# A state-space decoder layer: one GpSimd product for both half states, and a residual added by TensorE

## The chip, the cores and the metric

The kernel runs on one core of a Trainium2 chip. The metric is the device time of one execution in microseconds (us). The time before is the median of three runs; beside it there is one profiled execution, whose trace gives the times of single instructions. The core has five engines with a queue of instructions each: TensorE (PE, with its weight loads, PEld), VectorE (DVE), ScalarE (ACT), GpSimd (POOL) and SyncE (SP, which here issues DMA transfers). An engine works through its queue in order; it waits for another engine by a semaphore.

## What is computed

One decoder layer on x (4 sequences of 512 tokens, 256 channels) and a context of the same shape, all float32: a state-space network of two layers, cross-attention with 16 heads, and a mixture of 8 experts (the best 2 per token) beside a shared feed-forward part, each added to the stream.

```python
x = x + ssm(layernorm(x))
x = x + cross_attention(layernorm(x), ctx)
x = x + moe_and_shared(layernorm(x))

# one ssm layer; B and C have 16 states, xb has 512 channels
def scan_fn(carry, inp):
    h, v = carry
    dA_t, mi_t, C_t = inp
    v = BETA * v + mi_t            # BETA = 0.6
    h = dA_t * h + v
    return (h, v), jnp.einsum('ben,bn->be', h, C_t)
...
y = (y + dp * xb) * silu(z)
return jnp.einsum('ble,de->bld', y, ow)     # added to the layer's input
```

Here dA = exp(delta * A) and mi = delta * B * xb, for each of 512 channels, 16 states and 512 tokens of a sequence. The change touches the product of h with C, its sum over the states, and the last addition of the second layer: its output, the first layer's, and the x from outside.

## The kernel before

**Phases.** The state-space phase runs from the kernel's start to about 1214 us, the attention to about 1500, the experts to the end. Only the first is changed. In it, the stream of all four sequences stays in SBUF as `xs`, and the order of instructions is written out by hand (the function carries `manual_schedule`): what each engine's queue holds, and in what order, is the order in the program.

**Steps, pairs, units.** The work is cut into 8 steps, one for each layer and sequence: first layer 0 with its four sequences, then layer 1. Each step has 4 blocks of 128 channels (e), each block 2 pairs (q = 0 and 2), so there are 64 pairs. A pair covers two quarters of 32 channels (j = 0, 1). The 128 partitions of a tile hold 4 groups of 32: the same 32 channels with four of the 16 states. Four indices n = 0..3 thus make up the 16 states. A pair is 5 units, in an order given by the string `TURNS` (L59; "ffhfh" in four pairs of a step, then "fhfhf" in three, "hfhff" in the last).

- An *f* unit is a whole: one n from 1 to 3 with both quarters, in tiles of 128x1024 (two times 512 tokens). ScalarE makes the decay exp(delta * A) (L693), GpSimd the drive m = dxs * B (L702), VectorE scans v = 0.6 v + m into PSUM (L738) and then h = decay * h + v into SBUF (L747). GpSimd multiplies h by C in place (L760).
- An *h* unit is a half: n = 0 with one quarter, 128x512. Here v is not scanned. TensorE makes it as a product with a band of powers of 0.6 (`filtered`, 40 small products at L720) in the single PSUM buffer `vf`, and VectorE scans `hh` from it (L735). GpSimd multiplies it by C (L760 too). The half with js == (0,) is called `early`; the other one follows two units later.

Each f or each pair of halves ends as two products of TensorE with `joined` (L774), which add the four groups of states into the 32 rows of y in PSUM. TensorE does them one unit after the product with C or later: `sums` empties the list `pending`, and holds it back in the first units of each block until the block before has been gated (`finished`, L787: z = y * z on VectorE).

**Order within a unit.** The main loop's body is: decay of three groups ahead (ScalarE), drive of two wholes ahead (GpSimd), scans (VectorE), product with C (GpSimd), the bands' products for the unit two ahead, a piece of a background generator, the sums of what is pending (TensorE). The background generator is the next step's prologue: norm, input projection (L383), convolution (L499), the small matrices, the softplus. Where a projection is open, it goes before the background.

**Buffers.** m, h and hh are taken from the pool `ring3`, three buffers under each name. The tile framework makes a scan wait until the readers of the buffer that it gets are done.

**Projections.** After a step's last block has been gated, `projected` (L796 to L818) is done in the first units of the next step, in two rounds of two blocks of 128 tokens each. A round is eight products of TensorE into the PSUM tile `po` (L807; the trace has 16 records for them), then VectorE's cur += po (L816) on the stream's slice `cur`. In layer 1, GpSimd then adds the x from outside: cur += xt (L818). `xt` is loaded by SP at L802, when the projection begins, into a buffer shared with the softplus (`pre1`, tag "w"). In this phase layer 1 is projected for sequences 0 to 2, in the steps that begin at about 784, 924 and 1064 us; sequence 3's projection is done in the attention's code, which the change does not touch. `ident` is the 128x128 identity matrix, which the prologue uses for transposes and sums.

Of the kernel before, what the change touches and what calls it, by code (L numbers as in the profile page):

```python
# [10 lines left out]
F32 = mybir.dt.float32  # L11
I32 = mybir.dt.int32
AF = mybir.ActivationFunctionType
ALU = mybir.AluOpType
# [3 lines left out]
P = 128  # L18
B, L, D = 4, 512, 256
KD = D // P  # L20
TB = L // P
NL = 2
# [45 lines left out]
def decoder_layer(  # L68
# [26 lines left out]
    nc = tc.nc  # L95
# [7 lines left out]
    ident = const.tile([P, P], F32, name="ident")  # L103
# [106 lines left out]
    with ExitStack() as ph:  # L210
# [7 lines left out]
        pre6 = ph.enter_context(tc.tile_pool(name="ssm_pre6", bufs=6))  # L218
        ring2 = ph.enter_context(tc.tile_pool(name="ssm_ring2", bufs=2))
        ring3 = ph.enter_context(tc.tile_pool(name="ssm_ring3", bufs=3))  # L220
        ps_beta = ph.enter_context(tc.tile_pool(name="ssm_ps_beta", bufs=1, space=PSUM))
        ps_v = ph.enter_context(tc.tile_pool(name="ssm_ps_v", bufs=1, space=PSUM))
        ps_vf = ph.enter_context(tc.tile_pool(name="ssm_ps_vf", bufs=1, space=PSUM))
# [439 lines left out]
        for i in range(len(pairs)):  # L663
            ns, js = iter(range(1, SQ)), iter(((0,), (1,)))
# [42 lines left out]
        left = []  # L707

        filtering = {}

        def filtered(u):

# [16 lines left out]
        def scanned(u):  # L729
            i, n, js = units[u]  # L730
            dA = decaying[i, n][:, js[0] : js[-1] + 1, :]
            if n == 0:
                v = filtering.pop(u)
                h = ring3.tile([P, L], F32, name="hh")
                nc.vector.tensor_tensor_scan(h, dA[:, 0, :], v, 0.0, ALU.mult, ALU.add)  # L735
                return h.unsqueeze(1)
            v = ps_v.tile([P, 2, L], F32, name="v")
            nc.vector.tensor_tensor_scan(  # L738
                v.rearrange("p n t -> p (n t)"),
                beta.rearrange("p n t -> p (n t)"),  # L740
                entering.pop(u).rearrange("p n t -> p (n t)"),
                0.0,
                ALU.mult,
                ALU.add,
            )
            h = ring3.tile([P, 2, L], F32, name="h")
            nc.vector.tensor_tensor_scan(  # L747
                h.rearrange("p n t -> p (n t)"),
                dA.rearrange("p n t -> p (n t)"),
                v.rearrange("p n t -> p (n t)"),  # L750
                0.0,
                ALU.mult,
                ALU.add,
            )
            return h

        def weighted(u, h):
            i, n, js = units[u]
            Cs = made[pairs[i][0]][3][1]
            nc.gpsimd.tensor_tensor(h, h, Cs[n].unsqueeze(1).to_broadcast([P, len(js), L]), ALU.mult)  # L760
            return h

        def summed(u, *hcs):
# [32 lines left out]
        def projected(s, z):  # L796

            l, b = s
            outw = weights[l][5][0]
            if l == NL - 1:  # L800
                xt = pre1.tile([P, TB, D], F32, tag="w", name="xt")
                nc.sync.dma_start(xt, blocks(x[b]))  # L802
            for t in range(0, TB, 2):
                po = ps.tile([P, 2, D], F32, tag="mm", name="po")
                for i in range(2):
                    for k in range(NE):
                        nc.tensor.matmul(  # L807
                            po[:, i, :],
                            z[k // 2][:, k % 2, (t + i) * P : (t + i + 1) * P],
                            outw[:, k, :],  # L810
                            start=(k == 0),
                            stop=(k == NE - 1),
                        )
                yield
                cur = xs[:, b, t : t + 2, :]
                nc.vector.tensor_tensor(cur, cur, po, ALU.add)  # L816
                if l == NL - 1:
                    nc.gpsimd.tensor_tensor(cur, cur, xt[:, t : t + 2, :], ALU.add)  # L818


        DOUBLE = (8, 23, 38), (8, 13, 18, 23, 30, 33, 38)
# [23 lines left out]
        pending = []  # L845
# [74 lines left out]
        for u, (i, n, js) in enumerate(units):  # L920
            s, e, q = pairs[i]
            if u % 16 == 15 and empty < NX * ROWS + SPARE * P:
                empty = emptied(empty)
            if u % 16 == 7:
                next(fillers, None)
            if u % per == 0 and (e, q) == (0, 0):
                k = steps.index(s)
                if k == 0:
                    background = chained(background, prologue(*steps[1], s))
                    foreground = None  # L930
                else:
                    for _ in background:
                        pass
                    if s == (1, 0):
                        load_others(1)
                    if k + 1 < len(steps):
                        background, foreground = prologue(*steps[k + 1], s), None
                    else:
                        background, foreground = kept_from(), gates(s)

                fetching = k > 0 and k + 1 < len(steps) and steps[k + 1][0] == 0
                if fetching:
                    next(background)
                slot = 0
            if s == (1, 0) and slot == 10:
                load_last(1)
            if u in groups and groups.index(u) + LEAD < len(groups):
                later = groups[groups.index(u) + LEAD]
                i2 = units[later][0]
                if later % per == 0 and i2 + 1 < len(pairs):  # L950
                    while pairs[i2 + 1] not in stored:
                        next(background)
                    copied(i2 + 1)
                owed.append(later)
            between = units[u - 1][1:] == (0, (0,))
            while owed and not between and (n > 0 or 0 in js):
                decayed(owed.pop())
            if n > 0 and wholes.index(u) + AHEAD < len(wholes):
                driven(wholes[wholes.index(u) + AHEAD])
            gating = 3 if TURNS[i // 2 * 2 % len(TURNS)][1] == "h" else 2  # L960
            if u % per == gating and q == 0 and u > per:
                finished(*pairs[i - 1][:2])
            h = scanned(u)
            if projections:

                if n > 0 and next(projections[0], s) is s:
                    projections.pop()
            elif slot > 1 and foreground is not None:
                if next(foreground, s) is s:
                    foreground = None  # L970
            early = n == 0 and js == (0,)
            hc = weighted(u, h)

            def filters():
                if u + 2 < len(units) and units[u + 2][1] == 0:
                    s2, e2 = pairs[units[u + 2][0]][:2]
                    while (s2, e2 // 2) not in ready:
                        next(background)
                    filtered(u + 2)

            def sums():

                while pending and not 0 < slot % (2 * per) < gating:
                    summed(*pending.pop(0))

            if early:
                filters()
                sums()
                half = hc[:, 0, :]
            else:  # L990
                if n > 0:
                    filters()
                if 0 < slot <= 4 or not projections and foreground is None and not (fetching and slot == 0):
                    held = next(background, None)
                    if held is None and not projections and (
                        n > 0 and (k == 0 and slot < 20 or k == len(steps) - 1 or units[(u + 1) % len(units)][1] > 0) or slot in DOUBLE[k < len(steps) - 1]
                    ):
                        next(background, None)
                if n == 0:
                    filters()  # L1000
                sums()
                pending.append((u, hc[:, 0, :], hc[:, 1, :]) if n > 0 else (u, half, hc[:, 0, :]))
            if k + 1 < len(steps) and slot in (36, 38):
                spread(steps[k + 1], 0 if slot == 36 else 3)
            if slot == 36 and k + 1 < len(steps):
                bands = banded()
            if slot >= 36 and k + 1 < len(steps):
                for _ in range(2):
                    next(bands, None)
            slot += 1  # L1010
# [263 lines left out]
    with ExitStack() as ph:  # L1274
# [20 lines left out]
        for i in range(2):  # L1295

            t = wp.tile([P, TB, P], F32, name=f"tops{i}")
# [10 lines left out]
        xt = ring.tile([P, TB, D], F32, tag="wide", name="xt")  # L1308
# [74 lines left out]
        n = B * NG * 8  # L1383
        for s in range(-LEAD, n + 2):
            u, k = divmod(s, 8)
# [72 lines left out]
    with ExitStack() as ph:  # L1458
# [174 lines left out]
        for b in range(B):  # L1633
            for c in range(TOP):
                first = NB * P + (c * B + b) * L
                n = TB * D
# [20 lines left out]
        halves = {b: shared(b) for b in (2, 3)}  # L1657
# [70 lines left out]
```

## Time and profile before

| What | Value |
|---|---|
| median of 3 runs | 1793.54 us (1793.04 to 1795.99) |
| profiled execution | 1796.24 us, of which the span of its instructions is 1794.5 |
| mean granted TensorE clock | 0.938 |
| state-space phase | 60 to about 1214 us; 8 steps of about 140 us |
| GpSimd, h * C, 128x1024 (L760) | 192 times, 2361 ns each |
| GpSimd, hh * C, 128x512 (L760) | 128 times, 1279 ns each |
| GpSimd, m = dxs * B, 128x1024 (L702) | 192 times, 2365 ns each |
| GpSimd, cur += xt, 128x512 (L818) | 6 times, 1275 ns each |
| VectorE, scans of v and of h, 128x1024 | 192 times each, 2281 and 2287 ns |
| VectorE, scan of hh, 128x512 (L735) | 128 times, 1205 ns each |
| VectorE, cur += po (L816) | 14 times, 689 ns each |
| TensorE, y with joined (L774) | 768 records, 629 ns each, for h and hh together |
| TensorE, po (L807) | 224 records, 379 ns each |

The page of a profile shows an execution from several sides: the busy share of each engine, the span in 40 slices, the chain of work that ended last, and groups of equal instructions. A group is written `out<-in`, with partitions x elements; the number behind `x` is how often it occurs, then come its busy time and the mean of one. "Idle before" is the time in which the engine stood still just ahead of these instructions, and the name behind the arrow is what ended it. A line of waits, `A <- B`, reads: A waited, and B's end released it. Busy times of products on TensorE overlap, since they are pipelined; how long a group of them takes is read from its first start to its last end.

### The profile page before, as it was taken

To read this page: it belongs to the slowest core of one execution; us is meant where nothing else is said; L and a number is where in the kernel's file an instruction comes from. 1 tells how busy PE (TensorE), PEld (TensorE's weight loads), DVE (VectorE), ACT (ScalarE), POOL (GpSimd) and SP (SyncE) were. 2 spreads that over 40 slices of the span, in tenths; PEclk is the share of its full clock that TensorE was granted. 3 is DMA by queue.
4 is the path that set the end of the run, shared out by engine and by line. 5 is a ranking of instruction groups with operands and counts; after the bars stand their busy time and mean duration, and the time that the engine had idled before them with its cause. 6 is when DMAs were issued, how large, how long until landed. Compare 5 with 4: busy or idle time off the path is not lost.

```text
span 1794.5 us, 28198 instructions
## 1 busy us (share of the span) xinstructions
PE 1564.6 (87%) x10666; PEld 736.6 (41%) x10666; DVE 1386.3 (77%) x1260; ACT 1028.3 (57%) x1613; POOL 1241.9 (69%) x781
## 2 busy tenths in 40 slices
PE   6679789779879879879979968877999999899998
PEld 2234343334334334334434334433233333466665
DVE  3588899989999999999999999985567676432223
ACT  4658767747876866876776765531444444412221
POOL 5598899989989999999999999982000211245540
PEclk9889999989999989989989989997999999899999
DMA  3433543543553653634554443633310100532214
GB/s 80 141 91 96 141 107 96 128 103 97 132 136 70 152 140 90 156 100 101 143 131 97 126 122 97 170 93 120 118 48 24 59 9 16 162 104 64 65 59 153
DMA packets 122991, 185.71 MB, mean 103 GB/s; under 512 B 19464, under 2 KB 58248, under 8 KB 122856
## 3 DMA queue, kind: packets, MB, share of 16 engines
q1 hardware_dynamic: 117576, 169.45, 35.9%
q0 software_dynamic: 5280, 14.46, 2.5%
q8 instruction: 85, 1.39, 0.3%
q14 instruction: 50, 0.41, 0.1%
HBM read 124.38 MB, written 59.46 MB: 102 GB/s over the span
## 4 chain that ended last, share of the span: by engine, by line
PE 58%; DVE 18%; ACT 10%; issue 7%; POOL 5%; DMA 2%; SPq 1%; DVEq 0%; another core or an unknown queue 0%; POOLq 0%; ACTq 0%
DVE v L738 8%; PE y L774 6%; PE sT L1424 6%; PE pc L499 5%; PE pp L383 5%; DVE h L747 5%; PE vf L720 4%; PE pu L1578 4%; PE sum L581 4%; PE pw L1601 4%; PE o L1337 3%; ACT decay L693 3%; PE sc L1424 3%; POOL h L760 2%; PE y L770 2%
## 5 line engine op out<-in xcount | busy, mean ns | idle before, releaser
L760 POOL TENSOR_TENSOR h<-h,Cs 128x1024 f32<-128x1024 f32 x192 | 453.3, 2361 | 53.3 <-DVE h L747 42.3
L702 POOL TENSOR_TENSOR m<-dxs,Bs 128x1024 f32<-128x1024 f32 x192 | 453.9, 2365 | 16.6 <-DMA deltas<-wide 16.6
L747 DVE TENSOR_TENSOR_SCAN h<-decay,v 128x1024 f32<-128x1024 f32 x192 | 439.1, 2287 | 17.7 <-DVE v L738 1.0
L738 DVE TENSOR_TENSOR_SCAN v<-beta,m 128x1024 f32<-128x1024 f32 x192 | 438.0, 2281 | 15.3 <-POOL m L702 10.4
L693 ACT ACTIVATE decay<-deltas,scaleA 128x511 f32<-128x511 f32 x512 | 332.7, 714 | 59.9 <-DVE h L747 58.9
L720 PE MATMUL vf<-band,dxT 106*32 106x102 f32 (+1 forms) x5120 | 184.2, 269 | 86.5 <-DVE hh L735 85.7
L1430 DVE TENSOR_REDUCE tops<-sc 128x2 f32<-128x1024 f32 x128 | 156.4, 1225 | 98.9 <-PE sc L1424 91.4
L774 PE MATMUL y<-h,joined 128*32 128x512 f32 x768 | 205.3, 629 | 27.3 <-POOL h L760 27.0
L720 PEld LDWEIGHTS vf<-band,dxT 106*32 106x32 f32 (+1 forms) x5120 | 145.4, 116 | 161.9 <-issue 110.9
L1435 ACT ACTIVATE at<-sT 128x1024 f32<-128x1024 f32 x128 | 128.8, 1024 | 140.1 <-PE sc L1424 100.1
L735 DVE TENSOR_TENSOR_SCAN hh<-decay,vf 128x512 f32<-128x512 f32 x128 | 154.2, 1205 | 29.2 <-PE vf L720 29.2
L760 POOL TENSOR_TENSOR hh<-hh,Cs 128x512 f32<-128x512 f32 x128 | 163.7, 1279 | 8.7 <-DVE hh L735 8.5
L113 POOL TENSOR_TENSOR rstd<-ve,neghalf 128x4 f32<-128x4 f32 x12 | 12.3, 1027 | 207.4 <-DVE ve L111 207.4
L1424 PE MATMUL sc<-kpad,qpad 32*128 32x512 f32 x512 | 145.1, 664 | 7.2 <-ACT at L1435 4.8
L1424 PE MATMUL sT<-q,kpad 32*128 32x512 f32 x512 | 139.1, 657 | 3.3 <-DVE q L1329 3.3
L383 PE MATMUL pp<-xnT,inw 128*128 128x512 f32 x256 | 124.1, 622 | 6.9 <-ACT z L658 3.4
L499 PE MATMUL pc<-xpad,taps 128*128 128x512 f32 x240 | 112.1, 604 | 0.0
L1610 POOL DMA_INDIRECT rows_out<-yg,target x39 | 40.0, 1026 | 78.8 <-DVE xgT L1571 68.6
L774 PEld LDWEIGHTS y<-h,joined 128*32 128x32 f32 x768 | 34.4, 112 | 137.4 <-issue 70.7
L1205 POOL DMA_INDIRECT rows_in<-row,at x32 | 31.8, 994 | 82.3 <-DVE stat L1218 39.6
L693 ACT ACT_TABLE_LOAD x62 | 79.5, 1283 | 5.2 <-DMA deltas<-wide 4.1
L1594 DVE COPY hgT<-pf 128x512 f32<-128x512 f32 x39 | 27.0, 692 | 69.1 <-PE pf L1592 69.1
(254 smaller groups left out, 2316.2 us busy)
## 6 DMA issues: line engine op xcount, KB each, us to landing
dxs<-wide SPq DMA_DIRECT2D x256, 128.0 KB
deltas<-wide SPq DMA_DIRECT2D x256, 128.0 KB
rows_in<-nothing SPq DMA_DIRECT2D x17, 1028.0 KB
Cs<-rows SPq DMA_DIRECT2D x128, 64.0 KB
wide<-w SPq DMA_DIRECT2D x16, 512.0 KB
wide<-ln SPq DMA_DIRECT2D x16, 512.0 KB
Bs<-rows SPq DMA_DIRECT2D x32, 192.0 KB
xt<-in_x_dram SPq DMA_DIRECT2D x8, 512.0 KB
```

The costliest lines, as they stand in the source:

```text
L383: nc.tensor.matmul(pp, weights[l][1][half][:, k, m * P : (m + 1) * P], xnT[:, k, :], start=(k == 0), stop=(k == KD - 1),)
L499: nc.tensor.matmul(pcs[j], taps[:, e, k, :], xpads[j][:, k : k + L], start=(k == 0), stop=(k == KC - 1),)
L693: nc.scalar.activation(dA[:, j, 1:], copies[i][0][:, j, 1:], AF.Exp, scale=weights[s[0]][6][:, e, q + j, n : n + 1])
L702: nc.gpsimd.tensor_tensor(m, copies[i][1], Bs[:, n - 1, :].unsqueeze(1).to_broadcast([P, 2, L]), ALU.mult)
L720: nc.tensor.matmul(v[r * QP : (r + 1) * QP, CHUNKS[c] : CHUNKS[c + 1]], made[s][5][e // 2][:k, c, first : first + QP], band[:k, c, r, : CH ...
L735: nc.vector.tensor_tensor_scan(h, dA[:, 0, :], v, 0.0, ALU.mult, ALU.add)
L738: nc.vector.tensor_tensor_scan(v.rearrange("p n t -> p (n t)"), beta.rearrange("p n t -> p (n t)"), entering.pop(u).rearrange("p n t -> p ...
L747: nc.vector.tensor_tensor_scan(h.rearrange("p n t -> p (n t)"), dA.rearrange("p n t -> p (n t)"), v.rearrange("p n t -> p (n t)"), 0.0, AL ...
L760: nc.gpsimd.tensor_tensor(h, h, Cs[n].unsqueeze(1).to_broadcast([P, len(js), L]), ALU.mult)
L774: nc.tensor.matmul(ys[s, e][(q + j) * QP : (q + j + 1) * QP, :], joined, hcs[j], start=False, stop=(u % per == per - 1),)
L1424: nc.tensor.matmul(o, l, m, start=True, stop=True)
L1430: nc.vector.tensor_reduce(top[:, t2, 2 * h : 2 * h + 2, HD : HD + 1], sc, AX.X, ALU.max, negate=True)
```

## The change

It has two parts.

1. The two half states of a pair go into the two halves of one tile `h` (128x2x512). Each half's scan writes its half; GpSimd multiplies nothing after the first, and the whole tile by C after the second. Tiles of halves and of wholes come from one pool `ring4` of four buffers with a common tag, instead of three for wholes and three for halves. The sums read the two halves of that tile.
2. In layer 1's projections in this phase, TensorE adds x to the sum in `po`: for each block of 128 tokens a product of `ident` with the block of `xt` goes first into the group. VectorE's addition of `po` to the stream stays, GpSimd's addition is gone.

```diff
+        ring4 = ph.enter_context(tc.tile_pool(name="ssm_ring4", bufs=4))
...
+        halves = {}
...
             if n == 0:
                 v = filtering.pop(u)
-                h = ring3.tile([P, L], F32, name="hh")
-                nc.vector.tensor_tensor_scan(h, dA[:, 0, :], v, 0.0, ALU.mult, ALU.add)
-                return h.unsqueeze(1)
+                if 0 in js:
+                    halves[i] = ring4.tile([P, 2, L], F32, tag="h", name="hh")
+                h = halves[i]
+                nc.vector.tensor_tensor_scan(h[:, js[0], :], dA[:, 0, :], v, 0.0, ALU.mult, ALU.add)
+                return h
...
-            h = ring3.tile([P, 2, L], F32, name="h")
+            h = ring4.tile([P, 2, L], F32, tag="h", name="h")
...
-            nc.gpsimd.tensor_tensor(h, h, Cs[n].unsqueeze(1).to_broadcast([P, len(js), L]), ALU.mult)
+            nc.gpsimd.tensor_tensor(h, h, Cs[n].unsqueeze(1).to_broadcast([P, 2, L]), ALU.mult)
...
                 for i in range(2):
+                    if l == NL - 1:
+
+                        nc.tensor.matmul(po[:, i, :], ident, xt[:, t + i, :], start=True, stop=False)
                     for k in range(NE):
                         nc.tensor.matmul(
...
-                            start=(k == 0),
+                            start=(k == 0 and l < NL - 1),
...
                 nc.vector.tensor_tensor(cur, cur, po, ALU.add)
-                if l == NL - 1:
-                    nc.gpsimd.tensor_tensor(cur, cur, xt[:, t : t + 2, :], ALU.add)
...
-            hc = weighted(u, h)
+
+            hc = h if early else weighted(u, h)
...
-                half = hc[:, 0, :]
...
-                pending.append((u, hc[:, 0, :], hc[:, 1, :]) if n > 0 else (u, half, hc[:, 0, :]))
+                pending.append((u, hc[:, 0, :], hc[:, 1, :]))
```

## The prediction

> **What bounds the kernel now.** I read the page first, then the waits by engine over the stretch that the change touches, then the chain of waits in one step, then the instructions in order of time around one projection.
>
> ```profile
> PE 1564.6 (87%) x10666; PEld 736.6 (41%) x10666; DVE 1386.3 (77%) x1260; ACT 1028.3 (57%) x1613; POOL 1241.9 (69%) x781
> ```
>
> Over the span no engine is full, but the state-space phase (60 to 1214 us) is 64% of it and has 64 pairs in 8 steps of 140 us. There GpSimd looks like the bound: 145.8 of 150 us busy between 690 and 840 us, with VectorE at 143.2 and TensorE at 130.9. The waits say otherwise. This is GpSimd from 540 to 1140 us:
>
> ```profile
> engine line waited for: us in total, times, longest us
> POOL h L760 <- DVE h L747: 16.0, 24, 1.7
> POOL hh L760 <- DVE hh L735: 1.0, 1, 1.0
> ```
>
> and this is VectorE over the same 600 us:
>
> ```profile
> engine line waited for: us in total, times, longest us
> DVE hh L735 <- PE vf L720: 10.3, 15, 1.1
> DVE z L787 <- PE y L774: 3.7, 4, 1.4
> DVE xs L816 <- PE po L807: 3.0, 5, 1.1
> DVE w L606 <- PE sum L581: 1.2, 4, 0.4
> DVE v L738 <- POOL m L702: 0.5, 1, 0.5
> ```
>
> GpSimd catches VectorE up and waits for it (17 us). VectorE waits for GpSimd 0.5 us, and for TensorE 18 us. So GpSimd is full, and follows; VectorE and TensorE set the pace in turns. The chain of waits for 656 to 705 us shows TensorE's turn:
>
> ```profile
> by line: PE y L774 22.3%; PE pp L383 21.8%; PE pc L499 17.0%; PE vf L720 15.0%; PE po L807 14.9%; PE y L770 6.2%; DVE hh L735 2.5%; PE pt L474 2.1%; issue 0.6%
> ...
> 663.35 3.65 PE po L807 x16
> 669.70 3.65 PE po L807 x16
> ```
>
> In a step TensorE first waits 7 to 10 us for a scan, then runs without a gap, and VectorE stops for it again and again (hh L735, z L787, xs L816). The projections, po, lie in just this stretch. In the step's second part TensorE waits for VectorE (vf L720 <- DVE hh, 3.0 to 3.2 us), and VectorE paces.
>
> **Part 1: one product for both halves.** Per pair GpSimd loses two products of 1.279 us and gets one of 2.361 (L760): 64 x (2.558 - 2.361) = 12.6 us less work. The engine that loses it is the one that waits for others, so I put this at nothing, with one exception. TensorE waits for a weighted state in a few places of its own stretch (0.89 us at 527.9, 0.58 at 816.9, 0.51 at 956.7), where GpSimd is late because of the first half's product, the small operations of the norm and L818. Those waits close. In layer 1's first step GpSimd works back to back from 521.9 us, the first half's 1.28 comes off and the second half's 1.08 goes on soon after, so only 0.2 remains. With as much in step 0, the gain is 0.4 us. The other two count in part 2.
>
> The cost is lateness: a pair's second half is ready 2.36 us after GpSimd begins instead of 1.28. Behind it in GpSimd's queue stand the next m and h; the m is made two scans ahead (it is ready 5 to 9 us early), and the sum on TensorE comes late anyway: the product that ended at 704 us would end at about 705, its counterpart in the next step at 805.1 was summed at 812.4. Nobody waits.
>
> At the phase's end nothing moves either: the last h is scanned to 1209.9, GpSimd waits 2.5 us for it, and no half is left.
>
> A page speaks for more. The Trainium skill (SBUF — State Buffer, "SBUF: two separate sides") says that GpSimd and VectorE share a pair of ports as an exclusive lock, which the later one waits for until the holder's instruction ends. Were it so here, freeing GpSimd would quicken the scans. The row:
>
> ```profile
> L747 DVE TENSOR_TENSOR_SCAN h<-decay,v x192: 2286/2287/2290, 64.0 to 1207.6; 128x1024 f32<-128x1024 f32 x192
> ```
>
> Shortest, median and longest lie within 4 ns, and the 1202.78 scan, during 1.87 us of GpSimd's idleness, took 2.29 as well. By the rule up to 12.6 us; by the row nothing. I take nothing (each scan takes one input from PSUM, so the rule's own condition, two SBUF inputs, isn't met).
>
> **Part 1, the buffers.** The half states move into the four buffers of the whole states. A scan must wait until the sum that last read its buffer has ended. In the kernel before, a pool hands out the buffer whose last reader comes first in the program (the addresses in the compiled program show it for the exponentials of L1434, which are read last in another order than they are made). With this order I went through all 256 uses against the times of the sums: the sums end 1 to 5 us early, except at the last pair of each step, where the first half's scan would wait 0.25 to 0.58 us (scan 765.82, sum of F1 in pair 6 ended 766.30). The same half's partner waits 1.1 us for vf at 772.73, which hides it: nothing.
>
> What stays are the waits as instructions. The start of h after v differs by what it waits for:
>
> ```profile
> 703.01 2.30 DVE L738 TENSOR_TENSOR_SCAN v<-beta,m 128x1024 f32<-128x1024 f32 x1
> 705.45 2.29 DVE L747 TENSOR_TENSOR_SCAN h<-decay,v 128x1024 f32<-128x1024 f32 x1
> 707.65 1.20 DVE L735 TENSOR_TENSOR_SCAN hh<-decay,vf 128x512 f32<-128x512 f32 x1
> 708.76 2.27 DVE L738 TENSOR_TENSOR_SCAN v<-beta,m 128x1024 f32<-128x1024 f32 x1
> 711.07 2.29 DVE L747 TENSOR_TENSOR_SCAN h<-decay,v 128x1024 f32<-128x1024 f32 x1
> ```
>
> 2.44 us start to start where h also waits on ScalarE and TensorE, 2.31 where on v alone. Over the phase the medians are 2.307 (v alone), 2.376 (ScalarE too), 2.430 (both), 2.402 (TensorE without ScalarE): TensorE's wait costs 0.054 to 0.095. 64 of 192 h have it. A state whose buffer was a half's must wait for a sum that stands behind the last vf already waited for, some 5 times a step: about 40 more, 2.2 to 3.8 us. Here too a page speaks against the row: VectorE: DVE Perf Modes, "The DRAIN you can't avoid", measured no cost of a semaphore after each operation; by it the sum is 0. The row measures this wait, so I take it; but half falls where VectorE waits for TensorE anyway. I take 1.6; ends 0 and 3.8.
>
> **Part 2: x through TensorE.** GpSimd loses six additions of 1.276 us (7.7 us, off the path as above). TensorE gets one product of 128x256 per block of tokens, with ident: 4 for each of the 3 batches projected in this phase. The row nearest is po itself: 16 records, 8 products, in 3.72 us, thus 0.465 each. Two go into each po: +0.93 us per po, +1.86 per step. VectorE's addition keeps its length and now follows a longer po. TensorE also waits for x, which formerly GpSimd read later. The loads land at 797.3, 937.7 and 1083.6, the products would start at 801.5, 941.3 and 1084.2: no wait, by 0.6 us in the third; if it were lost, some tenths. SP issues the same load in the same place.
>
> Does the stretch hide the 1.86? At step 5:
>
> ```profile
> 806.06 0.66 DVE L816 TENSOR_TENSOR xs<-xs,po 128x512 f32<-128x512 f32 x1
> ...
> 811.57 0.69 DVE L816 TENSOR_TENSOR xs<-xs,po 128x512 f32<-128x512 f32 x1 [0.24 <-PE po L807]
> 812.69 1.22 DVE L735 TENSOR_TENSOR_SCAN hh<-decay,vf 128x512 f32<-128x512 f32 x1 [0.43 <-PE vf L720]
> ```
>
> The first addition has nearly 0.9 us to spare (po ended 805.18), the second none: it and the hh behind it, whose vf is queued behind po, move by 1.86. Then TensorE wins back its wait for GpSimd (0.58): 1.28 stay. From 817 to 855.9 TensorE has no gap over 0.2 us; ScalarE waits there for it (3.7 us) and runs on without a gap, and VectorE waits for them (0.89, 0.73, 0.64, 0.45). So 1.28 arrive where VectorE takes over, and nothing wins them back. Step 6: 1.86 - 0.51 = 1.35. Step 7: its first po costs 0.53 (TensorE's next transposes waited 0.68 for the addition anyway), its second 0.93: 1.46. Sum 4.1; ends 0, were every wait elastic, and 5.6.
>
> **Sum.** 4.1 + 1.6 - 0.4 = +5.3 us. The profiled execution took 1796.24 us (span 1794.5 and 1.7 around it), so it would take 1801.5; the median of the runs is 2.7 lower: 1793.54 + 5.3 = 1798.8.
>
> **Rivals.** *GpSimd is the bound after all.* Its 97% speaks for it, its waits against. All of its work that goes would count: 12.6 + 7.7 = 20.3 us, 1773. Chance 0.10.
>
> *Everything is absorbed.* For it speaks that ScalarE's wait of 3.7 us after the projection could take up the 1.28, if VectorE's stops for ScalarE behind it didn't grow with it; against it that VectorE already stops four times for TensorE and ScalarE in that stretch, each time with less to spare. Of the sum the waits as instructions stay at half their value, 0.8 to 1: 1794.5, between 1791 and 1797. Chance 0.27.
>
> *The buffers stop VectorE (much slower).* If the four buffers are handed out in turn, a first half gets the half's buffer of the pair before, whose sum TensorE does late. From the trace the scans would wait 0.7 to 1.8 us in the first part of a step (scan at 723.30, sum ended 725.05) and 2.2 to 2.5 in its last pair (769.33 against 771.77). TensorE comes back to VectorE's pace between the two, so both count: some 4 us in each of 8 steps, +32: 1826. It decides as soon as a sum ends after the scan four buffers later. Against it stands the order shown above. Chance 0.08.
>
> **Numbers.** The forecast has 0.55, own range 1795.5 to 1804. A measurement of this kernel tells about 0.2% (3.6 us) from no change, thus 1790 to 1797.1. Faster: the first rival 0.10 and 0.02 of the second, 0.12. Same: 0.25 of the second and 0.10 of the forecast's lower end, 0.35. Slower: 0.45 of the forecast and the third rival's 0.08, 0.53. The range 1790 to 1806 leaves out the first and third rivals.
>
> **What would show it.** Right: L774 waits for h less at 817 and 957; L816's wait grows by about 1.9 us per step in layer 1; GpSimd's waits for h L747 grow by some 10 us over the phase; steps 0 to 4 keep 140 us within 0.5. Wrong: h L747 or the half scans waiting 1 us and more for y L774 (buffers), VectorE waiting for GpSimd, steps 0 to 4 shorter by 1.5 us (GpSimd bound), or po waiting for x.

## The result, and the profile after

The changed kernel takes 1806.58 us, the median of 7 runs (1801.15 to 1809.84), against 1793.57 for the kernel before (7 runs, 1793.04 to 1796.27). The ratio, taken over the runs of both, is 1.0064, 95% interval 1.0052 to 1.0075: 11.5 us slower, 9.3 to 13.5, thus about 1805.1. (The two medians lie 13.0 apart; what follows goes by the ratio.) The forecast was +5.3, 1798.8. The result lies at the upper edge of the stated range, 1790 to 1806, and above the forecast's own range, which ended at 1804. The direction was right, the size less than half. The profiled execution took 1806.58, with a span of 1804.9. In the code after, lines have moved by 1 to 7: L764 is h * C, L751, L742 and L739 are the scans of h, v and hh, L778 the sums, L814 po, L812 the new product of x, L823 cur += po.

Four views answer to those of before. The engines' line of the page:

```profile
PE 1573.4 (87%) x10690; PEld 740.0 (41%) x10690; DVE 1388.3 (77%) x1260; ACT 1026.6 (57%) x1613; POOL 1224.1 (68%) x711
```

GpSimd has 70 instructions and 17.8 us less, TensorE 24 products' records and 8.8 us more. The waits of GpSimd from 540 to 1140 us:

```profile
engine line waited for: us in total, times, longest us
POOL h L764 <- DVE h L751: 39.1, 31, 3.9
...
POOL hh L764 <- DVE hh L739: 0.8, 2, 0.4
```

17.0 us of waiting for VectorE have become 39.9. The freed time went into waits, as the forecast had it. VectorE over the same stretch:

```profile
engine line waited for: us in total, times, longest us
DVE hh L739 <- PE vf L722: 10.2, 15, 1.6
DVE xs L823 <- PE po L814: 6.9, 7, 1.9
DVE z L791 <- PE y L778: 6.1, 2, 3.9
DVE hh L739 <- PE y L778: 2.6, 4, 0.8
DVE w L607 <- PE sum L582: 1.8, 6, 0.4
DVE h L751 <- PE y L778: 1.4, 2, 0.7
```

The wait for po has grown from 3.0 to 6.9, and the two lines in which a scan waits for y are new: these are the waits for buffers, 4.0 us in all and never over 0.8. The projection of step 5, VectorE's instructions in order of time:

```profile
809.15 0.69 DVE L823 TENSOR_TENSOR xs<-xs,po 128x512 f32<-128x512 f32 x1 [0.19 <-PE po L814]
...
816.36 0.69 DVE L823 TENSOR_TENSOR xs<-xs,po 128x512 f32<-128x512 f32 x1 [1.93 <-PE po L814]
817.51 1.22 DVE L739 TENSOR_TENSOR_SCAN hh<-decay,vf 128x512 f32<-128x512 f32 x1 [0.46 <-PE vf L722]
```

The first addition hardly waits, the second waits 1.93 instead of 0.24, and the scan behind it moves with it. That is 1.69 us more, in the place where the forecast put 1.86.

**Where the time went.** I compared the start of the first scan of v in each step (the last scan's end for step 7):

```
step length, us        2      3      4      5      6      7   rest
before              143.6  140.2  139.7  140.2  139.9  145.6  584.7
after               143.8  143.2  139.6  143.4  143.2  147.6  583.2
```

Steps 5 and 6 grew by 3.2 and 3.3, where the forecast had 1.28 and 1.35; step 7 by 2.0 (forecast 1.46). Step 3 grew by 3.0, but in later profiles it lies anywhere from 140.0 to 146.1 with and without each part of the change, and in a second profile of the changed kernel it has 140.0, so I don't count it. Steps 5 to 7 then show 8.5 of the 11.5 us; one profile cannot place the rest. Within step 5 the first scans are 3.17 us behind those of before at the start, 4.00 after the projection, 5.69 from unit 28 on (some 70 us after the projection) and 6.42 at the end. In step 6 the same places give 6.42, 7.59, 9.28 and 9.77. So the projection costs 0.8 and 1.2 us, and at unit 28, where the change altered nothing but buffers, 1.7 us are lost a second time.

What happens there is seen in TensorE's granted clock. The windows below are 3.41 us long; the columns are the busy time and instructions of TensorE, its weight loads, VectorE, ScalarE and GpSimd, then the granted clock, then DMA. Step 5 before:

```profile
864.16:867.58 3.42, 2.77 (x37) 1.50 (x27) 3.42 (x4) 2.20 (x6) 3.42 (x3) 1.00 0.19 50
867.58:870.99 3.41, 3.41 (x7) 0.78 (x8) 3.27 (x3) 3.41 (x7) 3.12 (x3) 0.50 0.79 195
870.99:874.40 3.41, 3.41 (x51) 1.84 (x48) 3.28 (x2) 3.30 (x5) 3.41 (x6) 1.00 0.89 194
```

and after:

```profile
867.61:871.03 3.42, 2.77 (x42) 1.78 (x39) 3.42 (x4) 2.23 (x6) 2.89 (x3) 1.00 0.50 110
871.03:874.44 3.41, 3.41 (x5) 0.57 (x3) 3.38 (x2) 3.36 (x6) 3.41 (x2) 0.50 0.60 159
874.44:877.85 3.41, 3.41 (x13) 0.76 (x14) 3.17 (x3) 3.38 (x5) 3.41 (x2) 0.50 0.95 206
877.85:881.27 3.42, 3.42 (x44) 1.99 (x41) 3.42 (x3) 3.37 (x4) 3.42 (x7) 1.00 0.95 250
```

The clock is 1.00 or 0.50, nothing between, and within each profile all its stretches at 0.50 start on a grid of 3.413 us and last one or more of its meshes (the last one, at the kernel's end, excepted). In both kernels TensorE has one mesh with 0.65 us of idleness. Before, one mesh at half clock follows; after, two. A mesh at half clock costs up to half of its length, 1.7 us, of TensorE's work. The instructions of TensorE in the changed kernel show what the mesh holds and what runs slowly:

```profile
863.39 3.63 PE L525 MATMUL pd<-xb,xpw 128*48 128x512 f32 x8
...
869.53 0.46 PE L557 MATMUL pb<-ident,dbc 48*106 48x48 f32 x5 [0.65 <-ACT dbc L530]
869.92 2.75 PE L552 MATMUL pa<-dbc,dtw 16*128 16x512 f32 x4
872.60 2.08 PE L774 MATMUL y<-xb,diagD 128*128 128x512 f32 x2
874.61 2.78 PE L778 MATMUL y<-h,joined 128*32 128x512 f32 x6
```

TensorE waits 0.65 us for ScalarE's copy dbc, then goes on, from 871.03 to 877.85 at half clock. The sums of y at 874.61 take 2.78 us. The kernel before has the same six records here, and its half clock ends in their midst:

```profile
865.54 0.46 PE L556 MATMUL pb<-ident,dbc 48*106 48x48 f32 x5 [0.66 <-ACT dbc L529]
...
870.04 1.94 PE L774 MATMUL y<-h,joined 128*32 128x512 f32 x6
```

TensorE sets the pace here. In both kernels the chain of waits runs from these transposes, pb, through TensorE's products alone to the addition w on VectorE, which stands still for it. Before:

```profile
884.36 0.69 DVE L606 TENSOR_TENSOR w<-sum,xb 128x512 f32<-128x512 f32 x1 [0.17 <-PE sum L581]
```

and after:

```profile
890.05 0.69 DVE L607 TENSOR_TENSOR w<-sum,xb 128x512 f32<-128x512 f32 x1 [0.17 <-PE sum L582]
```

From pb's start to w's start it takes 18.8 us before and 20.5 after, and these 1.7 us are those that are lost at unit 28.

### The profile page after: what moved, and what is told of

Same layout as the page of the kernel before. It is cut to its first block, busy times and chain, and to the rows that moved or that the text cites. A ratio compares the mean times of both kernels' runs of the same rounds, so it can differ in the third digit from the quotient of the medians.

```text
span 1804.9 us, 28182 instructions
## 1 busy us (share of the span) xinstructions
PE 1573.4 (87%) x10690; PEld 740.0 (41%) x10690; DVE 1388.3 (77%) x1260; ACT 1026.6 (57%) x1613; POOL 1224.1 (68%) x711
## 4 chain that ended last, share of the span: by engine, by line
PE 64%; DVE 16%; ACT 8%; issue 7%; DMA 2%; POOL 1%; SPq 0%; DVEq 0%; ACTq 0%; POOLq 0%
PE y L778 8%; DVE v L742 7%; PE sT L1429 6%; PE pp L384 6%; PE pc L500 5%; PE vf L722 5%; DVE h L751 4%; PE sum L582 4%; PE pu L1583 4%; PE pw L1606 4%; PE o L1342 3%; PE sc L1429 3%; ACT decay L694 3%; PE po L814 2%; PE y L774 2%
## 5 line engine op out<-in xcount | busy, mean ns | idle before, releaser
L764 POOL TENSOR_TENSOR h<-h,Cs 128x1024 f32<-128x1024 f32 x192 | 452.2, 2355 | 84.1 <-DVE h L751 72.2
L751 DVE TENSOR_TENSOR_SCAN h<-decay,v 128x1024 f32<-128x1024 f32 x192 | 439.0, 2287 | 22.2 <-PE y L778 2.2
L742 DVE TENSOR_TENSOR_SCAN v<-beta,m 128x1024 f32<-128x1024 f32 x192 | 437.9, 2281 | 15.0 <-POOL m L703 10.1
L778 PE MATMUL y<-h,joined 128*32 128x512 f32 x768 | 208.5, 638 | 23.8 <-POOL h L764 23.7
L1440 ACT ACTIVATE at<-sT 128x1024 f32<-128x1024 f32 x128 | 128.8, 1023 | 139.7 <-PE sc L1429 107.6
L739 DVE TENSOR_TENSOR_SCAN hh<-decay,vf 128x512 f32<-128x512 f32 x128 | 154.2, 1205 | 27.1 <-PE vf L722 23.2
L764 POOL TENSOR_TENSOR hh<-hh,Cs 128x1024 f32<-128x1024 f32 x64 | 150.7, 2355 | 5.0 <-DVE hh L739 5.0
L1615 POOL DMA_INDIRECT rows_out<-yg,target x39 | 39.9, 1023 | 78.6 <-DVE xgT L1576 70.7
L778 PEld LDWEIGHTS y<-h,joined 128*32 128x32 f32 x768 | 34.9, 114 | 135.2 <-issue 64.7
L384 PEld LDWEIGHTS pp<-xnT,inw 128*128 128x128 f32 x256 | 48.5, 199 | 79.0 <-issue 63.8
```

The lines of the kernel that those rows point to most:

```text
L384: nc.tensor.matmul(pp, weights[l][1][half][:, k, m * P : (m + 1) * P], xnT[:, k, :], start=(k == 0), stop=(k == KD - 1),)
L739: nc.vector.tensor_tensor_scan(h[:, js[0], :], dA[:, 0, :], v, 0.0, ALU.mult, ALU.add)
L742: nc.vector.tensor_tensor_scan(v.rearrange("p n t -> p (n t)"), beta.rearrange("p n t -> p (n t)"), entering.pop(u).rearrange("p n t -> p ...
L751: nc.vector.tensor_tensor_scan(h.rearrange("p n t -> p (n t)"), dA.rearrange("p n t -> p (n t)"), v.rearrange("p n t -> p (n t)"), 0.0, AL ...
L778: nc.tensor.matmul(ys[s, e][(q + j) * QP : (q + j + 1) * QP, :], joined, hcs[j], start=False, stop=(u % per == per - 1),)
```

## Theories

**Clock.** The projection's delay of about 1 us shifts this wait of TensorE on the throttle's grid, and the place on the grid decides whether no, one or two meshes at half clock follow. By this theory the added work costs what the forecast said, and the rest is the shift. **Plain sum.** The forecast's account: only added work and waits count. **Others**: the buffers, and GpSimd as the bound, from the forecast's rivals.

To compare kernels I use the *place* of the wait: the start of the transposes pb behind it, less the start of a half-clock mesh, in meshes of 3.413 us, whole meshes taken away. Before: 0.40 in step 5 and 0.36 in step 6. After: 0.57 and 0.58.

## Experiments

### The change again, and its parts

The first kernel is the changed one, unaltered. Then part 1 alone (projections as before), part 2 alone (scans, products and buffers as before), and part 1 with two products:

```diff
-            nc.gpsimd.tensor_tensor(h, h, Cs[n].unsqueeze(1).to_broadcast([P, 2, L]), ALU.mult)
+            part = h[:, js[0] : js[-1] + 1, :]
+            nc.gpsimd.tensor_tensor(part, part, Cs[n].unsqueeze(1).to_broadcast([P, len(js), L]), ALU.mult)
...
-            hc = h if early else weighted(u, h)
+            hc = weighted(u, h)
```

> The changed kernel once more, unaltered, beside its parts. The median should again be 1801 to 1810 us, 8 to 13 above the kernel before. Clock theory (TensorE's granted clock falls to a half in stretches of 3.4 us after it has idled, and the change moves or lengthens these stretches): the stretches of the second profile lie at the same places in the program give or take one or two, and where a stretch is missing the units behind it come 1 to 2 us earlier. Plain sum theory (only the work added to TensorE counts): no unit moves by over 0.5 us between the two profiles.

> Part 1 alone: both halves in one tile, one product of GpSimd, four common buffers; x is added by GpSimd as before. The forecast's sum: +1.2 us (0 to 3.4). Clock theory: +2 to +4, nearly all of it in the step that begins at 504 us, where the changed kernel lost 3.0 us with a new stretch at half clock, and nothing in steps 5 to 7. Rival, GpSimd is the bound: 12 us faster than before.

> Part 2 alone: TensorE adds x, GpSimd's addition goes; halves as before. The forecast's sum: 1.86 us per step in steps 5 to 7 less what TensorE wins back, +4.1 in all. Clock theory: 3 us and more in each of steps 5 and 6, +7 to +9 in all, with the loss in two places of a step, at the projection and again some 60 us later, where a stretch at half clock is longer than before.

> Part 1's tiles and its four common buffers, but GpSimd multiplies each half when it is there, in two products of 128x512 as before; x is added by GpSimd. If part 1's cost is in the buffers and the waits on TensorE's sums, it is as slow as part 1 alone. If it lies in the one product that comes later, this is equal to the kernel before within 1 us. Forecast: the waits cost 1.6, so +1.6 here.

| Kernel | Ratio to before, 95% | us | Steps 3, 4, 5, 6, 7 in the profile |
|---|---|---|---|
| the change again | 1.0084 (1.0063 to 1.0105) | +15.1 | 140.0, 139.6, 143.4, 143.2, 147.6 |
| part 1 | 1.0010 (1.0001 to 1.0020) | +1.8 | 143.2, 139.7, 140.4, 140.0, 146.3 |
| part 2 | 1.0016 (1.0004 to 1.0028) | +2.9 | 146.0, 140.2, 140.2, 139.9, 146.7 |
| part 1, two products | 1.0005 (0.9996 to 1.0014) | +0.9 | 143.4, 139.9, 140.3, 140.0, 146.1 |

(The us are the ratio's distance from 1, times the median of the kernel before on the same chip, here 1793.4, in the tables below 1792.8 or 1794.0.) The parts cost 1.8 (0.2 to 3.6) and 2.9 (0.7 to 5.0), the forecast said 1.2 and 4.1; their sum is 4.7, the forecast's 5.3. But together they cost 11.5 or 15.1. What is missing lies in steps 5 and 6, which are 143.4 and 143.2 us long in both profiles of the change and about 140 with either part. Neither my theory's numbers for the parts nor the plain sum had this: I expected part 2 alone to carry the excess. Part 1 is not 12 us faster, so GpSimd isn't the bound; the version with two products can't be told from it, so the merging itself is worth nothing either way.

The grid explains why the parts don't add. With part 1 the wait's place is 0.25 and 0.39, with one mesh behind it as before. With part 2 it is 0.62 and 0.59, and **no** mesh follows. This is the window of step 5 with part 2:

```profile
869.70:873.11 3.41, 2.76 (x47) 1.75 (x40) 3.41 (x4) 2.44 (x6) 3.15 (x2) 1.00 0.43 97
873.11:876.53 3.42, 3.42 (x17) 0.93 (x17) 3.39 (x2) 3.16 (x6) 3.42 (x3) 1.00 0.58 137
```

The same 0.65 us of idleness, and the clock stays at 1.00. In step 5, part 2's scans come 1.2 us later after the projection, as forecast, and win back 1.4 at unit 28. With both parts the wait falls 0.01 to 0.05 meshes earlier than with part 2 alone, 0.05 to 0.2 us, and that is on the other side of the edge.

### Moving the wait with more work, and with less

If the place decides, more work can make the changed kernel faster, and less work can make part 2 slower. The first two kernels lay one product more at the head of each layer 1 projection, in the changed kernel and in the one before; the last leaves out one of part 2's four products.

```diff
                 po = ps.tile([P, 2, D], F32, tag="mm", name="po")
+                if l == NL - 1 and t == 0:
+                    nc.tensor.matmul(po[:, 0, :], ident, outw[:, 0, :], start=True, stop=True)
```

> The changed kernel with one product more on TensorE: each of layer 1's three projections begins with a product of 128x256 that the next one overwrites, about 0.45 us. Clock theory: in the changed kernel the wait of TensorE about 82 us into steps 5 and 6 lies at 0.57 of the throttle's grid of 3.41 us, where it is followed by two windows at half clock; from 0.60 on (part 2 alone) it is followed by none. 0.45 us more moves it to 0.70, so the windows go and each of the two steps becomes 2 to 3 us shorter, although it does more work: about 1801 to 1803, 4 to 6 below the changed kernel. Plain sum theory: 1.3 us slower than the changed kernel, 1808 to 1809.

> The kernel before with the same product more in layer 1's three projections, 0.45 us each. Clock theory: the wait moves from 0.36 to 0.40 of the grid, with one window at half clock behind it, to 0.50 to 0.53, with two: steps 5 and 6 become 1.5 to 2.1 us longer each, +3 to +4.5 in all, and step 7 by 0.5. Plain sum theory: +0.5 to +1.3 in all.

```diff
-                    if l == NL - 1:
-
+                    if l == NL - 1 and t + i > 0:
                         nc.tensor.matmul(po[:, i, :], ident, xt[:, t + i, :], start=True, stop=False)
...
-                            start=(k == 0 and l < NL - 1),
+                            start=(k == 0 and (l < NL - 1 or t + i == 0)),
```

> Part 2 alone with less work: x is left out of the first of the four token blocks of each projection in layer 1, so each has three products with the identity and not four, 0.45 us less of TensorE. Clock theory: part 2's wait at 0.60 to 0.62 of the grid, with no window at half clock behind it, moves to 0.47 to 0.50, where two follow: steps 5 and 6 grow from 140.1 to 142.5 to 143.5 us although they do less, and the whole is 4 to 6 us slower than part 2. Plain sum theory: 0.5 to 1.3 us faster than part 2.

| Kernel | Ratio to before, 95% | us | Step 5: place, meshes at half clock, length | Step 6 |
|---|---|---|---|---|
| before | | | 0.40, one, 140.2 | 0.36, one, 139.9 |
| the change (both profiles) | 1.0064, 1.0084 | +11.5, +15.1 | 0.57, two, 143.4 | 0.58, two, 143.2 |
| the change, longer | 1.0025 (1.0013 to 1.0036) | +4.5 | 0.68, none, 140.5 | 0.78, none, 139.9 |
| before, longer | 0.9989 (0.9977 to 1.0000) | -2.0 | 0.28, one, 140.4 | 0.30, one, 140.0 |
| part 2 | 1.0016 (1.0004 to 1.0028) | +2.9 | 0.62, none, 140.2 | 0.59, none, 139.9 |
| part 2, shorter | 1.0033 (1.0022 to 1.0044) | +5.9 | 0.53, two, 143.0 | 0.42, two, 143.2 |

The longer change is faster than the change, by 7.0 us against its first measurement and 10.6 against its second, more than the 4 to 6 expected; the intervals lie apart. The place is 0.68 where 0.70 was expected. This is its step 5:

```profile
865.96:869.37 3.41, 2.77 (x51) 1.81 (x44) 3.41 (x4) 2.66 (x6) 2.87 (x2) 1.00 0.54 126
869.37:872.79 3.42, 3.42 (x16) 0.94 (x16) 3.38 (x2) 2.93 (x5) 3.42 (x3) 1.00 0.56 155
```

The shorter part 2 has the two meshes, and comes out slower than part 2 although it does less:

```profile
864.19:867.60 3.41, 2.76 (x42) 1.82 (x39) 3.41 (x4) 2.19 (x6) 3.17 (x3) 1.00 0.30 71
867.60:871.02 3.42, 3.42 (x6) 0.59 (x6) 3.39 (x2) 3.42 (x6) 3.42 (x2) 0.50 0.65 156
871.02:874.43 3.41, 3.41 (x16) 0.75 (x20) 3.17 (x3) 3.38 (x5) 3.09 (x7) 0.50 0.97 209
```

Its steps 5 and 6 grew by 2.8 and 3.3, as expected; the whole rose by 3.0 and not by 4 to 6; its step 7 came out shorter (145.4 against 146.7). The intervals of the two kernels overlap a little, so here it is the steps that decide, and the direction of the whole agrees. The plain sum, which had less work made faster and more work slower, does not survive these two kernels.

The rule of the place can be read off far more often than in steps 5 and 6. Each profile has this wait of 0.65 us in six steps, 1 to 6. In the ten kernels that leave it unfilled these are 60 waits, and they sort without an exception: one mesh at half clock from 0.95 over 0 to 0.40, two from 0.42 to 0.58, none from 0.59 to 0.89. At two of the three edges the waits on either side are 0.01 meshes apart, 0.05 us.

The scatter of step 3 goes with such a mesh in another place. In all nine profiles in which it is 142.8 us or longer, a mesh at half clock lies about 25 or 35 us after its start, behind a wait of TensorE for GpSimd's h; in the five with 140.0 to 140.6 none does. The three at 146 have two meshes behind the wait for dbc besides. Why the mesh comes in some executions only is open: the changed kernel has it in one profile of two. The changed kernel's mesh at 539.9:

```profile
539.92 1.92 PE L778 MATMUL y<-h,joined 128*32 128x512 f32 x4 [2.13 <-POOL h L764]
```

and the same products before, at full clock:

```profile
538.42 1.05 PE L774 MATMUL y<-h,joined 128*32 128x512 f32 x4 [1.06 <-POOL h L760]
```

The longer kernel before didn't do what I expected. Its wait comes 81.24 us after the start of step 5, against 81.27 before: the 0.45 us never reached it. In the kernel before, TensorE waits 0.58 us for GpSimd's state soon after the projection; with the product that wait is gone, so it took the product up. So this kernel doesn't test what 0.45 us of delay does, only shows that the first 0.5 us of work in the projection are free; in the forecast this is the term that I subtracted.

### Filling TensorE's waits

If the wait itself brings the half clock on, products that nobody reads should keep it off. One filling of 0.5 us goes in the wait for dbc, another of 6.5 us in the long wait at each step's start:

```diff
             pb = bank("pb")
+            nc.tensor.matmul(pb[:, :D], ident, xb[0][:, :D], start=True, stop=True)
...
+                    if k > 0 and slot == 2:
+                        warm = ps.tile([P, L], F32, tag="mm", name="warm")
+                        for _ in range(7):
+                            nc.tensor.matmul(warm, ident, made[s][1][0], start=True, stop=True)
                     filtered(u + 2)
```

> The changed kernel with one product of 128x256 (about 0.47 us, overwritten by the next one) in TensorE's wait of 0.65 us for ScalarE some 82 us into each step, ahead of the five small transposes L557. It costs the path nothing. Clock theory: if it is the idle time that brings on the half clock there, the two windows behind it go or become one in steps 5 and 6, and each becomes 1.5 to 3 us shorter: 3 to 6 below the changed kernel. If the throttle weighs the small products around the wait rather than the wait, nothing changes. Plain sum theory: equal to the changed kernel within 0.5 us.

> The kernel before with seven products of 128x512 (about 6.5 us, into a bank that nothing reads) in TensorE's wait of 7.5 to 11.5 us in the third unit of steps 1 to 7. Clock theory: TensorE then keeps its full clock, where before 3 to 7 us of work behind the wait ran at a half: 1 to 3 us less per step, 10 to 18 in all, and steps 5 and 6 fall below 140 us. Rival, the half clock costs nothing since VectorE paces: equal to the kernel before, or 1 to 3 us slower where the products delay the next vf.

> The changed kernel with both fillings: seven products of 128x512 in TensorE's wait at the start of steps 1 to 7, one of 128x256 in its wait for ScalarE 82 us into each step. In the kernel before, the first filling brought TensorE 1.6 us per step forward, and there it then waited 1.61 us for GpSimd's weighted state; part 1 and part 2 took that wait away. If so, the filling counts here: 1 to 2 us less per step than with the second filling alone (1799.4), 1786 to 1793. If it still comes to nothing: 1799 to 1800, and another engine sets the step.

> Part 1 alone with both fillings; x is added by GpSimd. By the same account TensorE gains 1.5 us or more per step and has no 1.28 us per step of part 2 to carry: 3 to 4 us below the changed kernel with the fillings, 1782 to 1790, faster than the kernel before. If GpSimd binds once TensorE is quicker: equal to the kernel before within 2 us.

> The kernel before with both fillings, the control for part 1 with them. If GpSimd's two products per pair take back what TensorE wins, 1789 to 1793, slower than part 1 with the fillings by 3 us or more. If the fillings alone make the gain, equal to part 1 with them within 2 us.

| Kernel | Ratio to before, 95% | us | Mean granted clock | Steps 3, 4, 5, 6, 7 |
|---|---|---|---|---|
| the change, wait for dbc filled | 1.0038 (1.0024 to 1.0051) | +6.8 | 0.938 | 143.3, 139.6, 140.2, 139.8, 147.5 |
| before, start filled | 1.0001 (0.9990 to 1.0012) | +0.2 | 0.957 | 140.5, 139.1, 140.4, 140.1, 145.6 |
| the change, both filled | 0.9992 (0.9980 to 1.0004) | -1.4 | 0.953 | 146.1, 136.9, 139.9, 139.8, 147.0 |
| part 1, both filled | 1.0002 (0.9990 to 1.0015) | +0.4 | 0.952 | 140.6, 136.6, 141.8, 144.1, 147.6 |
| before, both filled | 0.9992 (0.9978 to 1.0006) | -1.4 | 0.955 | 142.8, 137.0, 142.6, 140.3, 145.9 |

The first row brings steps 5 and 6 back to 140 us at a place of 0.57 in step 5, where the unfilled change had two meshes at half clock:

```profile
866.42:869.83 3.41, 3.39 (x44) 2.04 (x41) 3.41 (x4) 2.26 (x6) 2.88 (x3) 1.00 0.44 102
869.83:873.25 3.42, 3.42 (x17) 0.91 (x17) 3.39 (x2) 3.33 (x6) 3.42 (x3) 1.00 0.61 162
```

In step 6 the wait had moved to 0.62, where none follows anyway. With that filling the change costs 6.8 us, close to the forecast's 5.3. But idleness is not the whole cause. The same profile has the filled wait in step 4, at 0.12, and there a mesh at half clock still follows one in which TensorE stood still for 0.01 us:

```profile
726.49:729.90 3.41, 3.40 (x13) 1.30 (x11) 3.38 (x4) 2.19 (x6) 3.41 (x2) 1.00 0.17 40
729.90:733.31 3.41, 3.41 (x14) 0.76 (x14) 3.31 (x2) 3.41 (x7) 3.41 (x3) 0.50 0.99 226
```

In the four kernels with this filling there are 24 filled waits. Half clock follows 11 of them, at the same places as without filling: one mesh from 0.95 over 0 to 0.40, two at 0.42 to 0.44. Only the two at 0.50 and 0.57 differ, with none where two would follow.

The filling at the start keeps the clock up and yet gains nothing in the kernel before. TensorE's line there shows where the gain goes:

```profile
794.53 1.09 PE L720 MATMUL vf<-band,dxT 104*32 104x104 f32 x40 [1.48 <-DVE hh L735]
...
805.32 3.72 PE L807 MATMUL po<-outw,z 128*128 128x256 f32 x16 [0.45 <-DVE xs L816]
...
815.40 1.05 PE L774 MATMUL y<-h,joined 128*32 128x512 f32 x4 [1.61 <-POOL h L760]
```

vf takes 1.09 us instead of 1.93, and TensorE then stands still for VectorE (0.45) and for GpSimd's state (1.61). With part 1 that last wait should have been shorter, and the filling should have counted. It is not: with both fillings TensorE waits there 1.78 and 1.76 us in steps 5 and 6 with part 1, and 1.60 and 1.61 in the kernel before. Step 4 is 137 us in all three kernels with both fillings, the kernel before included, so part 1 isn't what makes it; no half clock follows the filled wait in this step. In other steps the gain is lost again, and two meshes at half clock follow the filled wait in three of those: step 3 of the change (146.1), step 6 of part 1 (144.1), step 5 of the kernel before (142.6). No version beats the kernel before beyond its interval. My expectation for part 1 with fillings, 1782 to 1790, was wrong (1794.2), and so was the 10 to 18 us that the filling at the start should have gained.

## Why the prediction was right in sign and short in size

**GpSimd follows.** Right for its load. Without 17.8 us of its work nothing got faster, and its waits took the time (17.0 to 39.9 us, where some 10 more were said). Its lateness is another matter, see below.

**The merged product is worth nothing.** Right within the intervals: part 1 with one product or two is the same. Two clauses on the way to it were wrong. "Those waits close": with part 1 alone TensorE still waits 0.47 and 0.66 us for GpSimd's h in steps 5 and 6, where it was 0.58 and 0.51; only with part 2 are these waits gone. "Nobody waits" for the later product: in step 3 TensorE does, 2.13 us instead of 1.06 (lines above), and 1.78 in the second profile of the change.

**Scans aren't slowed by a busy GpSimd.** Right. The scan of h has the same mean with GpSimd less busy:

```profile
L751 DVE TENSOR_TENSOR_SCAN h<-decay,v 128x1024 f32<-128x1024 f32 x192 | 439.0, 2287 | 22.2 <-PE y L778 2.2
```

**Buffers.** Right in the main. The waits are 0.5 to 0.8 us in the last pair of a step, with one more of 0.7 at 96 us into steps 5 and 6, mostly given back one scan later. The rival of 32 us is out.

**Waits as instructions.** Right. Scans of h that start within 2.36 us of their v fell from 70 to 39; the summed spacing from v to h grew by 1.8 us with part 1, a little under the 2.2 to 3.8 of the forecast before halving. Part 1 measured +1.8, the forecast +1.2, and the interval of 0.2 to 3.6 can't tell them apart.

**Part 2 in the projection.** Right in place and near in size: 1.93 us of waiting at the second addition, and a delay of 0.8 and 1.2 us behind it where 1.28 and 1.35 were said. x never kept TensorE waiting. That part 2 alone measured 2.9 us, near the 4.1, is luck in part: its steps 5 and 6 are as long as before (140.2 and 139.9), though the forecast had 2.6 us of its sum there.

**"So 1.28 arrive where VectorE takes over, and nothing wins them back."** This step failed. Between the projection and that point the forecast took TensorE's clock as given. The trace of before showed a half-clock mesh there, at 867.6 us, which a shift by 1.28 us could remove, leave or double. With part 2 alone it was removed, and the delay was won back. With both parts it was doubled, 1.7 us more in each of two steps. The sum lacked this term: 3.4 us against before, in two steps that grew by 3.2 and 3.3. Against the two parts' own profiles steps 5 and 6 of the change are 6.2 us longer than their costs added up; by the medians the change costs 6.8 us more than the sum of its parts, or 10.4 in the second measurement. That the excess comes from the place, and not from the work, is shown by the kernels that moved the place: with more work steps 5 and 6 fell back to 140 us, and with less they rose to 143.

What stays open is why these places have two, one or no mesh at half clock. The wait's 0.65 us are not needed, as the filled waits show. The products around the wait use few rows or columns of the array (16*128, 128*48, 128*32), and which of them share its mesh differs; a kernel that changes only their shape was not tried. The Trainium skill (TensorE: Matmul & The Clock Gate, "Part 1: The HAM clock gate") has a window of 3413 ns, which agrees with the grid's 3.413 us here. It has the clock fall after about a whole idle window; here it fell after meshes with 0.65 us of idleness, and after some with 0.01, and the measurement decides. Where the rest of the fillings' gain went stays open too. That steps cluster at 140 and 143.3 us, close to 41 and 42 meshes, suggests that steps lock to the grid; that is argued, not shown.

## What to carry to other kernels

Work added to or taken from an engine is worth what it moves on the path, and for GpSimd at 97% less load moved nothing: read who waits for whom. Where TensorE paces and its granted clock drops in the profile near the change, put the next half-clock stretches into the range: here a shift of 0.05 to 0.2 us decided over 3 us per step. Judge small changes by several placements of the same work, since one placement measures the grid as much as the change.

## What was not expected of the hardware

More work made a kernel faster: 0.45 us of products in three places took 7 us or more off the change. Less work made one slower: three products fewer lengthened two steps by 2.8 and 3.3 us, and the whole by 3.0, where the intervals overlap a little. The half clock came without the wait: a mesh in which TensorE was busy for 3.40 of 3.41 us was followed by one at 0.50. And a mean clock of 0.957 instead of 0.938 left the kernel before at the same time.
